# Order of the last feed-forward: steps written together, oldest group first, with a pause behind each combination of statistics

## The chip, the cores and the metric

The kernel runs on one core of one Trainium2 chip. Its time is the device time in microseconds of one execution, and the number that counts is the median of several runs. A separate execution under the hardware profiler gives the trace from which all durations here are taken.

## What is computed

The input is `x`, 4 images of 128 channels by 64 x 64 pixels. Layer 0 (a 1x1-convolution block with spatial attention) and the attention of layer 1 come first and take most of the time. What the change touches is the feed-forward half of layer 1 for the last image, for each of its 4096 tokens of 128 channels, cut here to what matters:

```python
def _ln(v, g, b):
    mu = jnp.mean(v, axis=-1, keepdims=True)
    var = jnp.mean((v - mu) ** 2, axis=-1, keepdims=True)
    return (v - mu) * jax.lax.rsqrt(var + EPS) * g + b
...
attn_out = ctx @ w_comb.T + b_comb
x1 = _ln(x + attn_out, g1, beta1)
zf = jnp.cos(x1[..., :NQ_FFN]) * jnp.cos(ry_theta)
h = jax.nn.relu(zf @ w1.T + b1)
ffn_out = h @ w2.T + b2
return _ln(x1 + ffn_out, g2, beta2)
...
t = t + _L1_attn_ref(...)
t = t + _L1_ffn_ref(_ln_t(t), ...)
```

So each token passes three normalisations (the two `_ln` and the `_ln_t` before the last layer), a cosine of its first eight channels, and four products (with `w_comb`, `w1`, `w2`, and `W` of the last layer). The last layer is a batch normalisation over all tokens of all images, followed by a recurrence in time, `y = sigmoid(wx + y @ V.T)`; it can't begin before the products with `W` of all tokens have gone into the statistics.

## The kernel before, in words

The four images go one after the other through a first stage (convolutions and layer 0), a second stage (attention), and feed-forwards that run beside the next image's first stage. The last image has no image behind it: its feed-forwards are a stage of their own, `last_stage` (from line 1680). Behind it comes the recurrence, which begins with `norm_of_products` (line 1494).

`last_stage` has eight groups of 512 tokens, each a generator made by `last_feed_forward` (line 1310). They are called A to H here, in the order in which they begin. A tile of a group is 128 partitions by 512, four blocks of 128 tokens. The steps of a group, with the engine and the tile names of the profile, are:

- loads of `x1` and `x0` on SyncE's queue, transposes `pc` on TensorE; `cT`, a copy on ScalarE (L1350); the product `pw` on TensorE (L1355); its addition to `x1` on VectorE (L1365);
- `parts`: four `bn_stats` on VectorE into `st` (L1322);
- `deviation` and the mean, on GpSimd: six small operations (L1329 to L1334, the last a power of -1/2) and one more, from `st` to `sv`, `rv` and `mv`;
- `both`: four normalising operations on VectorE that read `mv` (L1339);
- the chain of eight small VectorE operations on `z`, `zk`, `zr` (L1378 to L1391), the sine on ScalarE (L1393), a cast and a subtraction on VectorE (L1395, L1397), two copies into `zs` on ScalarE (L1402), transposes `pz` on TensorE, `zT` on ScalarE (L1409);
- twice the product `ph` on TensorE (L1416) and `hT` on ScalarE (L1426); then the 32 matmuls of `pf` on TensorE (L1432);
- `both` with `rv` and `pf` on VectorE; `parts`; the combination on GpSimd into `su`, `ru`, `mu`; `both` with `mu`; `both` with `ru`, which gives `t2`;
- `parts` of `t2` on VectorE and its transposes `pt` on TensorE; the combination on GpSimd into `sw`, `rw` and `less`, while ScalarE copies `t2T` (L1468) and SyncE stores it;
- the normalisation on ScalarE (L283), transposes `pl` on TensorE, the copy `last` on ScalarE (L1476), the product `pwx` on TensorE (L1489), `bn_stats` into `wx_stats` on VectorE (L1480) and the copy to `every` on ScalarE (L1482).

TensorE, ScalarE, VectorE and GpSimd execute their instructions here in the order in which the program writes them (`manual_schedule`). That order comes from a loop over ticks at the end of `last_stage`. Group k begins at tick `begins[k]`, and each active group goes one step further per tick; a tick is a matter of the order of writing and no barrier on the chip. Some pieces of the attention's end are written at the start of certain ticks (`between`): among them 16 copies each on ScalarE (ticks 2 and 8), on VectorE (tick 2) and on GpSimd (ticks 6 and 9, `xs` at L979), and joins on VectorE (ticks 4, 7 and 12).

Within a tick the groups take turns. A `yield 1` ends a group's step; a `yield 0` hands over to the next active group inside the same tick, so that `parts`, `both` and the small chains of several groups are written alternately, one VectorE instruction of each:

```python
on = list(active)
while on:
    for g in list(on):
        end = next(g, None)
        if end is None:
            active.remove(g)
        if end != 0:
            on.remove(g)
```

A group has 30 steps. GpSimd's combination is one step, and the VectorE or ScalarE instructions that read its result are the next. Tiles are taken from pools in turn: eight PSUM banks (`ps_one`), ten `fhalf`, six `hT`, eight of each small one.

Of the kernel before, what the change touches and what calls it, by code (L numbers as in the profile page):

```python
# [26 lines left out]
def kernel(  # L27
# [57 lines left out]
    here = {}  # L85
# [1224 lines left out]
    def last_feed_forward(im, i):  # L1310

        n, cols = im["n"], ts(i, IC)
        bits, _ = here["bits"]

        def bit(name, *shape):
            return bits.tile([P, *shape], F32, tag=name, name=f"{name}{n}_{i}")

        def parts(ap, st):  # L1320
            for k in range(TG):
                nc.vector.bn_stats(st[:, k, :], ap[:, ts(k, P)])  # L1322
                yield 0

        def deviation(st, sums, r):

            d = bit("d", TG)
            tt, each = nc.gpsimd.tensor_tensor, nc.gpsimd.tensor_scalar
            tt(sums, st[:, :, 1:3], st[:, :, 4:6], ALU.add)  # L1329
            tt(d, st[:, :, 1], st[:, :, 4], ALU.subtract)  # L1330
            tt(d, d, d, ALU.mult)
            each(r, sums[:, :, 1], 4.0 / P, 4e-5, ALU.mult, ALU.add)
            tt(r, r, d, ALU.add)
            tt(r, r, minus_half[:, 0:TG], ALU.pow)  # L1334

        def both(out, in0, factors, in1, op0, op1):
            for k in range(TG):
                at = ts(k, P)
                nc.vector.scalar_tensor_tensor(  # L1339
                    out[:, at], in0[:, at], factors[:, k : k + 1], in1(at), op0, op1  # L1340
                )
                yield 0

        x1, x0 = get("x1", f"lx1_{i}"), get("x0", f"lx0_{i}")
        nc.sync.dma_start(out=x1, in_=im["x1"][:, cols])
        nc.sync.dma_start(out=x0, in_=im["x0"][:, cols])
        pt = transposed(blocks(im["q"][:, cols]), f"pc{n}_{i}")
        yield 1
        cT = get("fhalf", f"cT{n}_{i}")
        nc.scalar.copy(cT, pt)  # L1350
        yield 1
        pa = one_psum(f"pw{n}_{i}")
        bias_first(pa, 1)
        for k in range(TG):
            nc.tensor.matmul(  # L1355
                pa[:, ts(k, P)],
                cT[:, ts(k, P)],
                wc_sb,
                start=False,
                stop=True,  # L1360
                skip_group_check=True,
            )
        yield 1
        v = x1
        nc.vector.tensor_tensor(v, pa, x1, ALU.add)  # L1365
        yield 1
        st = bit("st", TG, 6)
        yield from parts(v, st)
        yield 1
        sums, rv, mean = bit("sv", TG, 2), bit("rv", TG), bit("mv", TG)  # L1370
        deviation(st, sums, rv)
        nc.gpsimd.tensor_scalar(mean, sums[:, :, 0], 0.5, None, ALU.mult)
        yield 1

        yield from both(v, v, mean, lambda at: here["twice"][:, 0, :], ALU.subtract, ALU.mult)
        yield 1
        z, zk, zr = (bit(name, TG, D) for name in ("z", "zk", "zr"))
        nc.vector.tensor_tensor(  # L1378
            z, blocks(v)[:, :, 0:D], rv.unsqueeze(2).broadcast_to([P, TG, D]), ALU.mult
        )  # L1380
        yield 0
        nc.vector.tensor_tensor(z, z, be1_z.unsqueeze(1).broadcast_to([P, TG, D]), ALU.add)
        yield 0
        nc.vector.tensor_scalar(zk, z, 1.0 / (2 * math.pi), ROUND, ALU.mult, ALU.add)
        yield 0
        nc.vector.tensor_scalar(zk, zk, ROUND, None, ALU.subtract)
        for part, of in ((TWO_PI_1, z), (TWO_PI_2, zr), (TWO_PI_3, zr)):
            yield 0
            nc.vector.scalar_tensor_tensor(zr, zk, -part, of, ALU.mult, ALU.add)
        yield 0  # L1390
        nc.vector.scalar_tensor_tensor(zr, zr, -1.0, zr, ALU.mult, ALU.max)  # L1391
        yield 1
        nc.scalar.activation(zr, zr, AF.Sin, bias=half_pi, scale=-1.0)  # L1393
        yield 1
        nc.vector.tensor_copy(z.bitcast(F32R), zr)  # L1395
        yield 0
        nc.vector.tensor_tensor(zr, zr, z, ALU.subtract)  # L1397
        yield 1
        zs = get("fhalf", f"zs{n}_{i}")
        zv = zs.rearrange("p (k r y d) -> p k r y d", k=TG, y=2, d=D)  # L1400
        for y, part in enumerate((z, zr)):
            nc.scalar.copy(  # L1402
                zv[:, :, :, y, :], part.unsqueeze(2).broadcast_to([P, TG, P // (2 * D), D])
            )
        yield 1
        pz = transposed(blocks(zs), f"pz{n}_{i}")
        yield 1
        zT = get("fhalf", f"zT{n}_{i}")
        nc.scalar.copy(zT.bitcast(F32R), pz)  # L1409
        yield 1  # L1410
        hs = []
        for f0 in range(0, NF, 2):
            phs = [one_psum(f"ph{n}_{i}_{f}") for f in range(f0, f0 + 2)]
            hs.append(get("hT", f"hT{n}_{i}_{f0}"))
            for j in range(2):
                nc.tensor.matmul(  # L1416
                    phs[j],
                    f1_sb[:, f0 + j, :].bitcast(F32R),
                    zT.bitcast(F32R),
                    start=True,  # L1420
                    stop=True,
                )
            yield 1
            for j in range(2):
                bias = fb1_sb[:, f0 + j : f0 + j + 1]
                nc.scalar.activation(hs[-1][:, j, :], phs[j], AF.Relu, bias=bias)  # L1426
            yield 1
        po = one_psum(f"pf{n}_{i}")
        bias_first(po, 2)
        for k in range(TG):  # L1430
            for f in range(NF):
                nc.tensor.matmul(  # L1432
                    po[:, ts(k, P)],
                    hs[f // 2][:, f % 2, ts(k, P)],
                    f2_sb[:, f, :],
                    start=False,
                    stop=f == NF - 1,
                    skip_group_check=True,
                )
        yield 1  # L1440
        u = v
        yield from both(u, v, rv, lambda at: po[:, at], ALU.mult, ALU.add)
        yield 1
        st = bit("st", TG, 6)
        yield from parts(u, st)
        yield 1
        sums, r, mean = bit("su", TG, 2), bit("ru", TG), bit("mu", TG)
        deviation(st, sums, r)
        nc.gpsimd.tensor_scalar(mean, sums[:, :, 0], 0.5, None, ALU.mult)
        if i == NTG - 1:  # L1450
            nc.vector.tensor_tensor(blocks(x0), blocks(x0), row4(be2_bc), ALU.add)
        yield 1
        yield from both(u, u, mean, lambda at: here["twice"][:, 1, :], ALU.subtract, ALU.mult)
        yield 1
        t2 = x0
        yield from both(t2, u, r, lambda at: x0[:, at], ALU.mult, ALU.add)
        yield 1
        st = bit("st", TG, 6)
        yield from parts(t2, st)
        pt = transposed(blocks(t2), f"pt2_{n}_{i}")  # L1460
        yield 1
        sums, r, less = bit("sw", TG, 2), bit("rw", TG), bit("less", TG)
        deviation(st, sums, r)
        nc.gpsimd.tensor_tensor(less, sums[:, :, 0], r, ALU.mult)
        nc.gpsimd.tensor_scalar(less, less, -1.0, None, ALU.mult)
        nc.gpsimd.tensor_scalar(r, r, 2.0, None, ALU.mult)
        t2T = get("fhalf", f"t2T{n}_{i}")
        nc.scalar.copy(t2T, pt)  # L1468
        nc.sync.dma_start(out=t2_dram[im["rows"], cols], in_=t2T)
        yield 1  # L1470
        normalise_act(blocks(u), blocks(t2), less, r, TG)
        yield 1
        pt = transposed(blocks(u), f"pl{n}_{i}")
        yield 1
        tokens_i = get("fhalf", f"last{n}_{i}")
        nc.scalar.copy(tokens_i, pt)  # L1476
        yield 1
        pw = token_products(n, i, tokens_i)
        yield 1
        nc.vector.bn_stats(wx_stats[:, n * NIC + i, :], pw)  # L1480
        dst = held["every"][:, n, cols]
        nc.scalar.copy(  # L1482
            dst.rearrange("p (t c) -> p c t", t=L), pw.rearrange("p (c t) -> p c t", t=L)
        )
# [195 lines left out]
    def last_stage(im):  # L1680
# [28 lines left out]
        with stage(  # L1709
# [14 lines left out]
            while groups or active:  # L1724
                for f in between.get(tick, ()):
                    f()
                if groups and tick >= begins[NTG - len(groups)]:
                    active.append(groups.pop(0))
                on = list(active)
                while on:  # L1730
                    for g in list(on):
                        end = next(g, None)
                        if end is None:
                            active.remove(g)
                        if end != 0:
                            on.remove(g)
                tick += 1

    x_rows = x.rearrange("n c s -> (n c) s")
# [266 lines left out]
```

## Time and profile before

| | us |
|---|---|
| median of 3 runs (6988.06 to 6990.65) | 6988.64 |
| the profiled execution, its own time | 6989.88 |
| span of the profiled execution, first to last instruction | 6988.2 |
| busy in the span: TensorE / VectorE / ScalarE / GpSimd | 6812.8 / 5967.8 / 5932.7 / 2786.7 |
| last attention result of TensorE (L845) | up to about 6768.6 |
| first `wx_stats` of the last stage, last `wx_stats` of it (end) | 6846.7, 6892.4 |
| mean granted TensorE clock | 0.989 |

Times inside the trace count from the span's start. A line of the timeline gives start, duration, engine, line, operation, written and read tiles, shape, count, and in brackets the idle time before it and what ended that. Tile names leave out buffer numbers, and `lx` stands for the tiles of `x1`, `v`, `u`, `x0` and `t2`, which share buffers. A line of the waits view gives the waiting engine, tile and line, what it waited for, the total in us, how often, and the longest one.

### The profile page before, as it was taken

Reading aid. Unit: us, or ns where it says so; the run is one execution under the profiler, and the core shown is the slowest. Engines: PE = TensorE matmul, PEld = TensorE weight load, DVE = VectorE, ACT = ScalarE, POOL = GpSimd, SP = SyncE. Lnnn points to the kernel's source line nnn. Section 1 sums busy time; section 2 is a strip of 40 time slices with the busy share of each in tenths; the row PEclk is TensorE's granted clock in tenths of the full one; section 3 lists DMA queues with packets and bytes.
Section 4 is the critical chain, followed back from the end, with each engine's and each line's share of the span. In section 5 each row is a group of like instructions: output and inputs, shape, how many; then the busy total and the mean of one; then the engine's idle time right before and its main releaser. Section 6 shows DMA issues by size and latency. Waiting matters only on the chain. (4 is left out here: it accounts for less than half of the span.)

```text
span 6988.2 us, 223483 instructions
## 1 busy us (share of the span) xinstructions
PE 6812.8 (97%) x92333; PEld 3660.6 (52%) x92333; DVE 5967.8 (85%) x8064; ACT 5932.7 (85%) x11843; POOL 2786.7 (40%) x10008
## 2 busy tenths in 40 slices
PE   8999999999999999999999999999999999999996
PEld 4545555555664555555565455555466555555554
DVE  6688889987888999888787888888978888898987
ACT  4479999996669999999566999999956699999984
POOL 1134444434333444443433344444343434344442
PEclk9999999999999999999999999999999999999998
DMA  1110000000111000000111100000001100000012
GB/s 32 37 41 25 24 28 21 22 10 23 49 50 42 26 21 22 21 22 9 33 50 49 37 22 21 22 20 24 22 26 47 56 25 22 22 24 29 13 62 109
DMA packets 84760, 219.87 MB, mean 31 GB/s; under 512 B 9384, under 2 KB 10288, under 8 KB 82960
## 3 DMA queue, kind: packets, MB, share of 16 engines
q1 hardware_dynamic: 80448, 200.34, 8.4%
q8 instruction: 726, 11.89, 0.7%
q10 hardware_dynamic: 3024, 4.99, 0.2%
q14 instruction: 306, 2.51, 0.1%
q0 software_dynamic: 256, 0.13, 0.0%
HBM read 141.44 MB, written 56.62 MB: 28 GB/s over the span
## 5 line engine op out<-in xcount | busy, mean ns | idle before, releaser
L1069 ACT ACTIVATE e<-s 128x1024 f32<-128x1024 f32 (+1 forms) x3480 | 2950.0, 901 | 114.8 <-PE s L1057 83.0
L832 DVE STREAM_TRANSPOSE t<-e 128x1024 f32<-128x1024 f32 x2240 | 2594.2, 1210 | 77.3 <-ACT e L1069 74.6
L845 PEld LDWEIGHTS misc<-t,mirror 128*32 128x32 f32 x57344 | 1656.6, 110 | 1327.2 <-issue 1270.8
L845 PE MATMUL misc<-t,mirror 128*32 128x128 f32 x57344 | 1968.3, 273 | 18.6 <-DVE later L859 15.8
L1069 ACT ACTIVATE xs<-s 128x1024 f32<-128x1024 f32 (+1 forms) x2152 | 1838.9, 908 | 55.2 <-PE s L1057 43.0
L832 DVE STREAM_TRANSPOSE t<-xs 128x1024 f32<-128x1024 f32 x1344 | 1562.5, 1210 | 42.7 <-ACT xs L1069 41.2
L866 PE MATMUL acc<-e,q_aug 128*32 128x512 f32 x11360 | 1524.7, 609 | 1.0 <-POOL q_aug L748 1.0
L1057 PE MATMUL s<-queries,keys 32*128 32x512 f32 x9216 | 1243.2, 497 | 20.7 <-ACT e L1069 10.4
L912 POOL COPY own<-o 32x36 f32<-32x36 f32 x2048 | 430.7, 210 | 1807.1 <-DVE o L904 1727.1
L514 PE MATMUL acc<-p,asmT 128*128 128x512 f32 x2048 | 946.2, 593 | 1.8 <-DVE e L410 1.6
L866 PE MATMUL acc<-xs,q_aug 128*32 128x512 f32 x7072 | 942.4, 605 | 0.0
L507 ACT ACTIVATE p<-s 128x1024 f32<-128x1024 f32 x512 | 499.8, 1022 | 403.8 <-PE s L503 399.8
L1057 PEld LDWEIGHTS s<-queries,keys 32*128 32x128 f32 x9216 | 487.2, 182 | 601.4 <-issue 296.2
L937 POOL COPY other<-turned 32x64 f32<-32x64 f32 x1904 | 449.7, 236 | 624.3 <-DVE turned L927 545.8
L1069 ACT ACTIVATION_READ_ACCUMULATOR e<-s 128x1 f32 x2880 | 694.5, 241 | 0.0
L802 POOL COPY mirror<-q 32x128 f32<-32x128 f32 x2048 | 599.3, 293 | 199.2 <-PE misc L845 111.3
L503 PE MATMUL s<-hl,e 128*128 128x512 f32 x2048 | 586.4, 428 | 22.4 <-ACT p L507 10.9
L528 DVE TENSOR_TENSOR total<-total,p 128x1024 f32<-128x1024 f32 x448 | 547.8, 1223 | 22.0 <-ACT p L507 14.3
L514 PEld LDWEIGHTS acc<-p,asmT 128*128 128x128 f32 x2048 | 380.0, 190 | 334.8 <-issue 309.8
L503 PEld LDWEIGHTS s<-hl,e 128*128 128x128 f32 x2048 | 379.9, 189 | 178.3 <-issue 68.6
L1069 ACT ACTIVATION_READ_ACCUMULATOR xs<-s 128x1 f32 x1728 | 421.4, 244 | 0.0
L898 POOL COPY by_token<-by_key 32x4 f32<-32x4 f32 x2000 | 383.8, 192 | 84.4
(314 smaller groups left out, 4459.2 us busy)
## 6 DMA issues: line engine op xcount, KB each, us to landing
keys<-parts_dram SPq DMA_DIRECT2D x256, 256.0 KB
queries<-parts_dram SPq DMA_DIRECT2D x1024, 32.0 KB
x_dram<-x SPq DMA_DIRECT2D x56, 256.0 KB
fx<-x_dram SPq DMA_DIRECT2D x48, 256.0 KB
xs<-in_x_dram SPq DMA_DIRECT2D x16, 512.0 KB
t_dram<-t2T SPq DMA_DIRECT2D x32, 256.0 KB
t2s<-t_dram SPq DMA_DIRECT2D x16, 512.0 KB
hl<-hl SPq DMA_DIRECT2D x28, 256.0 KB
```

Of the source, the lines that this page charges most:

```text
L503: nc.tensor.matmul(s[:, j, :], stationary, moving, start=y == 0, stop=y == len(parts) - 1)
L507: nc.scalar.activation(p, s, AF.Exp)
L514: nc.tensor.matmul(state["acc", ic], asmT[:, ts(2 * jp + j, P)], p[:, j, :], start=jp == 0 and j == 0, stop=jp == NP - 1 and j == 1,)
L528: nc.vector.tensor_tensor(state[ic], state[ic], p, ALU.add)
L802: nc.gpsimd.tensor_copy(wv[ts(a, 32), s, :, :, ts(a, D)], own[ts(s, 32)])
L832: nc.vector.transpose(group["e"][h][:, k, :], es[h])
L845: nc.tensor.matmul(state["acc"][ts(2 * x + h, 32), :], state["w"][:, QT * (s // 4) + TG * x + s % 4, h, :], state["e"][h][:, :, ds(IC * x ...
L866: nc.tensor.matmul(it["in"]["acc"][ts(2 * h + x, 32), :], it["qa"][:, ds((2 * it["tiles"][x] + h) * V, 32)], it["e"][h][:, ts(x, IC)], sta ...
L912: nc.gpsimd.tensor_copy(own[ts(s, 32), ts(x, 4), h, :], ov[ts(2 * h + x, 32), s, :, 0:V])
L937: copy(to[ts(k, 32), h], tv[ts(2 * x + h, 32), k])
L1057: nc.tensor.matmul(ss[h][:, x, :], keys[unit[x] // QT].bitcast(F32R)[r, ts(unit[x] % QT, P)], queries[b].bitcast(F32R)[r, :], start=True, ...
L1069: nc.scalar.activation(es[h][:, ts(x, IC)] if split else es[h], ss[h][:, x, :] if split else ss[h].rearrange("p x c -> p (x c)"), AF.Exp, ...
```

## The change

Every `yield 0` goes, and each `yield 1` becomes a plain `yield`: what stands between two of them is written together. The loop lets each active group, the one that began first ahead of the others, go through one whole step per tick. Behind each of the three combinations on GpSimd a second `yield` is added, an empty step, so that a group has 33 steps and the instructions that read `mv`, `mu` and `rw` are written one tick later than before. `begins` and `between` stay as they are. No instruction is added, removed or changed. The transposes `pt`, which are in one step with `parts` of `t2`, were written behind four rounds of the tick and are now written with their group.

```diff
@@ -1320,7 +1320,6 @@
         def parts(ap, st):
             for k in range(TG):
                 nc.vector.bn_stats(st[:, k, :], ap[:, ts(k, P)])
-                yield 0
...
                 nc.vector.scalar_tensor_tensor(
                     out[:, at], in0[:, at], factors[:, k : k + 1], in1(at), op0, op1
                 )
-                yield 0
...
         st = bit("st", TG, 6)
-        yield from parts(v, st)
-        yield 1
+        parts(v, st)
+        yield
         sums, rv, mean = bit("sv", TG, 2), bit("rv", TG), bit("mv", TG)
         deviation(st, sums, rv)
         nc.gpsimd.tensor_scalar(mean, sums[:, :, 0], 0.5, None, ALU.mult)
-        yield 1
-
-        yield from both(v, v, mean, lambda at: here["twice"][:, 0, :], ALU.subtract, ALU.mult)
-        yield 1
+        yield
+        yield
+
+        both(v, v, mean, lambda at: here["twice"][:, 0, :], ALU.subtract, ALU.mult)
+        yield
...
-        yield 0
         nc.vector.tensor_tensor(z, z, be1_z.unsqueeze(1).broadcast_to([P, TG, D]), ALU.add)
-        yield 0
         nc.vector.tensor_scalar(zk, z, 1.0 / (2 * math.pi), ROUND, ALU.mult, ALU.add)
-        yield 0
...
         if i == NTG - 1:
             nc.vector.tensor_tensor(blocks(x0), blocks(x0), row4(be2_bc), ALU.add)
-        yield 1
-        yield from both(u, u, mean, lambda at: here["twice"][:, 1, :], ALU.subtract, ALU.mult)
-        yield 1
+        yield
+        yield
+        both(u, u, mean, lambda at: here["twice"][:, 1, :], ALU.subtract, ALU.mult)
+        yield
         t2 = x0
-        yield from both(t2, u, r, lambda at: x0[:, at], ALU.mult, ALU.add)
-        yield 1
+        both(t2, u, r, lambda at: x0[:, at], ALU.mult, ALU.add)
+        yield
         st = bit("st", TG, 6)
-        yield from parts(t2, st)
+        parts(t2, st)
         pt = transposed(blocks(t2), f"pt2_{n}_{i}")
-        yield 1
+        yield
...
         nc.sync.dma_start(out=t2_dram[im["rows"], cols], in_=t2T)
-        yield 1
+        yield
+        yield
         normalise_act(blocks(u), blocks(t2), less, r, TG)
...
                 if groups and tick >= begins[NTG - len(groups)]:
                     active.append(groups.pop(0))
-                on = list(active)
-                while on:
-                    for g in list(on):
-                        end = next(g, None)
-                        if end is None:
-                            active.remove(g)
-                        if end != 0:
-                            on.remove(g)
+                active = [g for g in active if next(g, active) is not active]
                 tick += 1
```

More of the change, by code (lines that the diff above doesn't have):

```diff
@@ L1380, in last_feed_forward @@
         )
-        yield 0
         nc.vector.tensor_tensor(z, z, be1_z.unsqueeze(1).broadcast_to([P, TG, D]), ALU.add)
-        yield 0
         nc.vector.tensor_scalar(zk, z, 1.0 / (2 * math.pi), ROUND, ALU.mult, ALU.add)
-        yield 0
         nc.vector.tensor_scalar(zk, zk, ROUND, None, ALU.subtract)
         for part, of in ((TWO_PI_1, z), (TWO_PI_2, zr), (TWO_PI_3, zr)):
-            yield 0
             nc.vector.scalar_tensor_tensor(zr, zk, -part, of, ALU.mult, ALU.add)
-        yield 0
         nc.vector.scalar_tensor_tensor(zr, zr, -1.0, zr, ALU.mult, ALU.max)
-        yield 1
+        yield
         nc.scalar.activation(zr, zr, AF.Sin, bias=half_pi, scale=-1.0)
-        yield 1
+        yield
         nc.vector.tensor_copy(z.bitcast(F32R), zr)
-        yield 0
         nc.vector.tensor_tensor(zr, zr, z, ALU.subtract)
-        yield 1
+        yield
         zs = get("fhalf", f"zs{n}_{i}")
@@ L1404, in last_feed_forward @@
             )
-        yield 1
+        yield
         pz = transposed(blocks(zs), f"pz{n}_{i}")
-        yield 1
+        yield
         zT = get("fhalf", f"zT{n}_{i}")
         nc.scalar.copy(zT.bitcast(F32R), pz)
-        yield 1
+        yield
         hs = []
@@ L1422, in last_feed_forward @@
                 )
-            yield 1
+            yield
             for j in range(2):
@@ L1426, in last_feed_forward @@
                 nc.scalar.activation(hs[-1][:, j, :], phs[j], AF.Relu, bias=bias)
-            yield 1
+            yield
         po = one_psum(f"pf{n}_{i}")
@@ L1439, in last_feed_forward @@
                 )
-        yield 1
+        yield
         u = v
-        yield from both(u, v, rv, lambda at: po[:, at], ALU.mult, ALU.add)
-        yield 1
+        both(u, v, rv, lambda at: po[:, at], ALU.mult, ALU.add)
+        yield
         st = bit("st", TG, 6)
-        yield from parts(u, st)
-        yield 1
+        parts(u, st)
+        yield
         sums, r, mean = bit("su", TG, 2), bit("ru", TG), bit("mu", TG)
@@ L1451, in last_feed_forward @@
             nc.vector.tensor_tensor(blocks(x0), blocks(x0), row4(be2_bc), ALU.add)
-        yield 1
-        yield from both(u, u, mean, lambda at: here["twice"][:, 1, :], ALU.subtract, ALU.mult)
-        yield 1
+        yield
+        yield
+        both(u, u, mean, lambda at: here["twice"][:, 1, :], ALU.subtract, ALU.mult)
+        yield
         t2 = x0
-        yield from both(t2, u, r, lambda at: x0[:, at], ALU.mult, ALU.add)
-        yield 1
+        both(t2, u, r, lambda at: x0[:, at], ALU.mult, ALU.add)
+        yield
         st = bit("st", TG, 6)
-        yield from parts(t2, st)
+        parts(t2, st)
         pt = transposed(blocks(t2), f"pt2_{n}_{i}")
-        yield 1
+        yield
         sums, r, less = bit("sw", TG, 2), bit("rw", TG), bit("less", TG)
@@ L1469, in last_feed_forward @@
         nc.sync.dma_start(out=t2_dram[im["rows"], cols], in_=t2T)
-        yield 1
+        yield
+        yield
         normalise_act(blocks(u), blocks(t2), less, r, TG)
-        yield 1
+        yield
         pt = transposed(blocks(u), f"pl{n}_{i}")
-        yield 1
+        yield
         tokens_i = get("fhalf", f"last{n}_{i}")
         nc.scalar.copy(tokens_i, pt)
-        yield 1
+        yield
         pw = token_products(n, i, tokens_i)
-        yield 1
+        yield
         nc.vector.bn_stats(wx_stats[:, n * NIC + i, :], pw)
```

## The prediction

> **What bounds the kernel now.** I read the windows view first, to size the stage that the change touches, then the waits inside it, then the timelines of VectorE (DVE), GpSimd (POOL) and TensorE. The stage runs from about 6770 us to the last `wx_stats` at 6892.43 us; behind it come the 94.5 us of the recurrence, which the change leaves alone. Columns: stretch, length, busy us of PE, PEld, DVE, ACT, POOL (with counts), granted clock, DMA share, GB/s.
> ```profile
> 6774.60:6893.50 118.90, 91.45 (x496) 72.45 (x495) 80.39 (x337) 66.16 (x143) 70.02 (x224) 0.77 0.23 91
> 6893.50:6988.00 94.50, 55.72 (x186) 29.42 (x186) 69.96 (x110) 36.47 (x93) 0.58 (x1) 0.81 0.45 172
> ```
> No engine is full in the stage, so waits decide. Here is the waits view of the stage.
> ```profile
> ACT every L1482 <- DVE wx_stats L1480: 18.3, 8, 3.5
> DVE lx L1339 <- POOL mu L1449: 13.8, 7, 3.4
> ...
> POOL sw L1329 <- DVE st L1322: 12.6, 6, 2.4
> ...
> DVE wx_stats L1480 <- PE pwx L1489: 10.1, 3, 3.6
> ...
> DVE lx L1339 <- POOL mv L1372: 7.1, 5, 2.4
> ...
> ACT lx L283 <- POOL rw L1466: 6.3, 2, 5.2
> ```
> VectorE and GpSimd wait for each other: VectorE 13.8 + 7.1 = 20.9 us for means from GpSimd (`mu`, `mv`), ScalarE 6.3 us for `rw`, and GpSimd 12.6 us for VectorE's `st`. The timelines of the two engines show the loop.
> ```profile
> 6854.40 0.22 POOL L1329 TENSOR_TENSOR sw<-st 128x8 f32<-128x8 f32 x1 [2.17 <-DVE st L1322]
> ...
> 6857.78 0.20 POOL L1329 TENSOR_TENSOR su<-st 128x8 f32<-128x8 f32 x1
> ...
> 6860.06 0.23 POOL L1449 TENSOR_SCALAR mu<-su 128x4 f32<-128x4 f32 x1
> ```
> ```profile
> 6852.27 0.35 DVE L1339 SCALAR_TENSOR_TENSOR lx<-lx,mu,twice 128x128 f32<-128x128 f32 x1 [2.13 <-POOL mu L1449]
> ...
> 6860.32 0.35 DVE L1339 SCALAR_TENSOR_TENSOR lx<-lx,mu,twice 128x128 f32<-128x128 f32 x1 [2.67 <-POOL mu L1449]
> ```
> From one `mu` to the next is 8.05 us: 2.1 us of VectorE up to the last `st`, then GpSimd's `sw` (3.4 us) and `su` (2.5 us) in series, for which VectorE stands still. The same eight microseconds lie at 6844.30 and 6868.30. At the end the last four groups follow at 4.33 us each (`wx_stats` at 6878.73, 6883.06, 6887.39, 6891.73): ScalarE's `every` 0.8 us, the next group's `last` 0.6, `pwx` 2.1 on a slow TensorE, `wx_stats` 0.7 and some 0.1 between them.
>
> **What the Trainium skill says.** "TensorE: Matmul & The Clock Gate", What's actually happening: the clock is halved after a mostly idle window of some 3.4 us and comes back after a busy one. The trace agrees; after TensorE sat 1.78 us for the first `pt`, the windows view has
> ```profile
> 6825.00:6828.00 3.00, 1.42 (x6) 0.82 (x7) 2.93 (x16) 2.15 (x5) 1.92 (x6) 1.00 0.00 0
> 6828.00:6831.00 3.00, 3.00 (x19) 3.00 (x18) 2.67 (x13) 0.79 (x2) 0.94 (x2) 0.61 0.25 93
> ```
> and that `pf` took 5.36 us where others take 3.73. A drop costs about 1.6 us. "VectorE: DVE Perf Modes", The DRAIN you can't avoid, says that chaining cannot skip the flush, and that an instruction that isn't held starts earlier. The trace has both: dependent small operations start 0.21 us apart (6786.38, 6786.59, 6786.81), interleaved with other groups' some 0.10 apart. "GPSIMD Engine Reference", Key points: GpSimd shares its SBUF interfaces with VectorE instructions of two SBUF inputs. The trace agrees: beside the 128x512 addition of L1451 a `sw` combination took 4.6 us instead of 3.3.
>
> **The change, part by part.** No instruction is added or removed; their order on VectorE, TensorE and ScalarE changes. A tick is no barrier, so an empty step costs nothing by itself.
>
> (1) *Steps together.* The small chain of `z` has eight operations. Alone it takes 1.67 us (6785.93 to 6787.60); interleaved it cost about 1.31 us (2.20 us from 6826.23 to 6828.43, less three big operations at 0.26 and one small at 0.11). The cast and subtraction cost 0.3 instead of 0.2. That is +0.45 us per group, and at most 8 x 0.45 = 3.6 us of VectorE, of which the first groups already pay. The big operations lose nothing: 0.20 us per `bn_stats`, 0.26 per normalising operation, in either order.
>
> (2) *The pause.* `mv`, `mu` and `rw` now have one further tick between GpSimd and their readers. VectorE's work then comes ahead: after the pause the even tick holds `ru` (1.04) and `parts` of u (0.80), the odd one `parts` of t2 (0.80), `mu` (1.04), `rv` (1.0), plus 0.6 for `wx_stats`; 5.3 us per two ticks. GpSimd needs 3.3 + 2.5 = 5.8. TensorE needs 5.55 while `pf` runs: `pf` 3.8, two `ph` 1.0, `pz` 0.35, `pt` 0.4. They overlap instead of adding up, so a two-tick round falls from 8.05 to about 5.6-6.4.
>
> (3) *`pt` moves ahead of the younger groups' TensorE work*, because it no longer comes after four rounds. It waits for the oldest group's `t2`. GpSimd's own queue keeps its order up to the first `su`; SyncE's only waiting issues are the eight stores of `t2T`, in the same order, and the 16 `t2s` loads wait for the end of the stage and shift with it.
>
> I followed the tick list engine by engine, in order, with those durations. Letters A to H are the groups.
> - Front. GpSimd's `sv` combinations and its two sets of 16 `xs` copies fill it from 6777.5 to 6794.8 in the old order. VectorE waits for the copies until 6785.0 as now, has A's normalisation and chain still to do, and is then full until `ru` of A at 6825.1. Before it waited some 6 us from there on (2.45, 0.36, 0.36, 0.34, 1.05, 1.76), but paid less for chains and had done A's normalisation inside the wait: A's `ru` started at 6825.85, and C's `rv` at 6829.25 where I now get 6825.1+1.04 = 6826.1. A gain of 1 to 3 us.
> - TensorE: `pf` of A, B, C at 6806.9, 6812.6, 6818.0 (now 6807.06, 6813.89, 6819.05). Then `pt` of A waits at the head of the queue from 6823.05 to 6824.8: one drop of clock, so D's `pf` ends at 6831.7 (now 6833.3).
> - From D on nothing waits for GpSimd. `pf` of E, F, G, H end at 6837.15, 6842.8, 6849.25 and 6854.75 (now 6840.88, 6847.99, 6854.37, 6861.26). ScalarE's 5.2 us at `rw` ahead of E's `hT` are gone.
> - Behind H's `pf`: `rv` 6855.0 to 6856.0, then in VectorE's order `ru` F, `parts` H, `parts` F, `mu` G, `wx_stats` C (1.04 + 0.8 + 0.8 + 1.04 + 0.6): C is done at 6860.3 (before: 6865.4).
> - Late next is the chain of 4.33 us per group, now for five groups rather than three: 6860.35 + 5 x 4.33 = 6882.0. Before: 6892.43. **Gain 10.4 us.**
> The profiled execution took 6989.88 us around its span of 6988.2, 1.24 above the median. 6989.88 - 10.4 = 6979.5; at the median 6988.64 - 10.4 = **6978.2 us**. Bounds of the parts that the trace doesn't show: the drop at `pt` costs 0 to 3.3 us (taken 1.6, one such drop seen); handovers I took at 0.1 to 0.25 us, as seen, and another 0.1 on some thirty of them makes 3 us. So 6975 to 6983 for this case. GpSimd has slack of 1.3 us (`su` of H, done 6860.8, wanted about 6862) to 5 us.
>
> **Rivals.**
> - *GpSimd stays the bound* (0.18). Five `sw` and six `su` lie between A's `sw` and H's `mu`. At 3.2 and 2.5 they take 31 us; at the 4.6 seen beside VectorE's two-input addition for each `sw`, 7 us more, less 1.3 of slack: 5.7 us late, **6984**. For: VectorE's normalising operations have two inputs and now run without gaps. Against: the page of the kernel before has such a slow `sw` once in eight.
> - *TensorE stays fast in the tail* (0.14). `pwx` then takes 1.0 instead of 2.1, five times: 5 us less, **6973**. For: `pt`, `pl`, `pwx` now lie together. Against: from 6866 to 6893 the clock was 0.50, with a busy share like that expected.
> - *Slower: `pt` at the head of TensorE's queue waits in every round* (0.10). Then each of D to H pays about 1 us of gap and 1.7 us of half clock: 5 x 2.7 = 13.5 us, **6992**, above today. It decides if VectorE's `ru` ends more than about a microsecond after TensorE is through, thus if VectorE needs more than 5.6 + 1 per two ticks; I count 3.6 to 5.3.
> - *Nothing gained* (0.06): the longer small chains in a full VectorE until 6826 take what the pauses give, **6988**.
>
> **How the numbers follow.** The likeliest case has 0.52 and gives the time. The range from 6971 to 6990 takes in the rivals but the slower one, and leaves some 0.15 outside. A measurement of this kernel can tell about 0.2% from no change, 14 us: under 6974.7 lies the fast tail, 0.14; above 7002.6 only a worse form of the slower rival, 0.04; the rest is 0.82.
>
> **What would show it.** Right: the waits of L1339 for `mu` and `mv` nearly gone; `mu` rounds of 5.6 to 6.4 us; `pf` of H ending near 6855; `wx_stats` 4.33 us apart from the third group on; stage end near 6882. Step (1) shows in the `z` chains, 1.67 us without a foreign instruction between. Wrong: `mu` still waiting, GpSimd without gaps (the first rival), or a clock of 0.5 between 6832 and 6855 with `pt` waiting for L1339 (the third).

## The result, and the profile after

The changed kernel takes 6975.85 us (median of 15 runs, 6973.11 to 6979.97), the kernel before 6988.06 us (15 runs, 6984.30 to 6990.65). The ratio is 0.9982, with a 95% interval of 0.9976 to 0.9989: 12.2 us less. The profiled execution took 6976.16 us around a span of 6974.4 us, against 6989.88 around 6988.2.

Totals of this kernel scatter by some 3 to 4 us to either side, and the work ahead of the last feed-forward has a part in it: in the traces below the stage begins between 6773.5 and 6779.0 us. Most of what follows is therefore read from the trace as **the stage**: from the first addition of `pw` on VectorE to the end of the last `wx_stats`. Two profiled executions of the changed kernel gave 105.64 and 105.69 us for it. In the kernel before it is 117.82 us (6774.61 to 6892.43).

The windows view of the changed kernel shows the stage and what is behind it, in the columns that the prediction names.

```profile
6774.46:6880.10 105.64, 83.09 (x494) 68.26 (x494) 80.94 (x336) 65.31 (x142) 68.60 (x224) 0.83 0.26 99
6880.10:6974.40 94.30, 55.95 (x188) 29.20 (x186) 70.80 (x111) 37.59 (x94) 0.58 (x1) 0.81 0.45 174
```

VectorE's busy time is about what it was (79.36 us before, from the same view with the same bounds): the stage is 12.18 us shorter because VectorE stands idle less (24.7 us instead of 38.5). The rest behind it, 94.30 us against 95.77, isn't touched by the change; in the other executions below it lies between 93.5 and 95.7 us.

The waits view of the stage in the changed kernel has no line in which VectorE waits for `mu` or `mv`, nor one in which ScalarE waits for `rw`; before these were 13.8, 7.1 and 6.3 us. Four of the lines that are left:

```profile
DVE wx_stats L1475 <- PE pwx L1484: 12.8, 4, 3.6
...
ACT every L1477 <- DVE wx_stats L1475: 8.8, 6, 2.9
...
DVE lx L1338 <- PE pf L1425: 4.0, 5, 1.3
...
PE pt L291 <- DVE lx L1338: 3.0, 1, 3.0
```

The first two lie mostly in the tail, in which each group's `wx_stats` waits for its `pwx`. The last is one wait of `pt` at the head of TensorE's queue, which the change brought.

How the loop of VectorE and GpSimd opened shows in their timelines. GpSimd first, in the changed kernel:

```profile
6847.28 0.22 POOL L1442 TENSOR_SCALAR mu<-su 128x4 f32<-128x4 f32 x1
6847.48 0.19 POOL L1328 TENSOR_TENSOR sw<-st 128x8 f32<-128x8 f32 x1
```

And VectorE:

```profile
6846.07 1.11 DVE L1338 SCALAR_TENSOR_TENSOR lx<-lx,mu,twice 128x128 f32<-128x128 f32 x4
...
6848.29 1.12 DVE L1338 SCALAR_TENSOR_TENSOR lx<-lx,rv,pf 128x128 f32<-128x128 f32 x4 [1.11 <-PE pf L1425]
...
6852.53 1.13 DVE L1338 SCALAR_TENSOR_TENSOR lx<-lx,mu,twice 128x128 f32<-128x128 f32 x4
```

The `mu` that GpSimd finishes at 6847.50 is read at 6852.53, 5 us later; `sw` starts as soon as `mu` is through, with no wait for `st`. VectorE now waits for TensorE's `pf` instead, and for less. From one `mu` on VectorE to the next is 6.46 us here, where it was 8.05.

Where the stage got shorter can be read group by group from the ends of `wx_stats`, counted from the stage's start:

| | A | B | C | D | E | F | G | H |
|---|---|---|---|---|---|---|---|---|
| before, us | 72.8 | 80.8 | 90.9 | 97.8 | 104.8 | 109.1 | 113.5 | 117.8 |
| after, us | 70.9 | 77.4 | 84.8 | 88.3 | 92.6 | 97.0 | 101.3 | 105.6 |
| gained, us | 1.9 | 3.4 | 6.1 | 9.6 | 12.2 | 12.2 | 12.2 | 12.2 |

All is gained by the fifth group. The three behind it still follow at 4.33 to 4.35 us each, as before. VectorE's timeline of the changed kernel has `wx_stats` of C, D, E and F:

```profile
6858.56 0.68 DVE L1475 BATCH_NORM_STATS2 wx_stats<-pwx 128x6 f32<-128x512 f32 x1
6862.03 0.68 DVE L1475 BATCH_NORM_STATS2 wx_stats<-pwx 128x6 f32<-128x512 f32 x1
6866.38 0.70 DVE L1475 BATCH_NORM_STATS2 wx_stats<-pwx 128x6 f32<-128x512 f32 x1 [1.84 <-PE pwx L1484]
6870.73 0.70 DVE L1475 BATCH_NORM_STATS2 wx_stats<-pwx 128x6 f32<-128x512 f32 x1 [3.65 <-PE pwx L1484]
```

C to D is only 3.47 us, then 4.35: D's `pwx` ran at full clock in 1.12 us, E's took 2.07. TensorE's timeline has both, and the gap that lies ahead of them:

```profile
6860.78 1.12 PE L1484 MATMUL pwx<-last,WT_sb 128*128 128x512 f32 x2 [3.53 <-ACT last L1471]
6864.27 2.07 PE L1484 MATMUL pwx<-last,WT_sb 128*128 128x512 f32 x2 [0.62 <-ACT last L1471]
```

### The profile page after: what moved, and what is told of

Same layout as the page of the kernel before. It is cut to its first block, busy times and chain, and to the rows that moved or that the text cites. A ratio compares the mean times of both kernels' runs of the same rounds, so it can differ in the third digit from the quotient of the medians.

```text
span 6974.4 us, 223486 instructions
## 1 busy us (share of the span) xinstructions
PE 6808.2 (98%) x92333; PEld 3655.8 (52%) x92333; DVE 5966.9 (86%) x8064; ACT 5937.1 (85%) x11843; POOL 2795.6 (40%) x10008
## 3 DMA queue, kind: packets, MB, share of 16 engines
q10 hardware_dynamic: 3024, 4.99, 0.2%
## 5 line engine op out<-in xcount | busy, mean ns | idle before, releaser
L503 PE MATMUL s<-hl,e 128*128 128x512 f32 x2048 | 587.7, 428 | 21.0 <-ACT hl L465 11.1
```

The lines of the kernel that those rows point to most:

```text
L503: nc.tensor.matmul(s[:, j, :], stationary, moving, start=y == 0, stop=y == len(parts) - 1)
```

## The experiments

Each was run beside the kernel before on one chip; e1 to e4, e0 with e5 to e7, and e8 to e11 are three sets on three chips. The table has what the traces show of each: the stage, the end of E's `wx_stats` from the stage's start (the loop), the time from there to the end of the stage (the tail of F, G, H), and VectorE's waits for `mu` and `mv` and ScalarE's for `rw`. Each stage is that of one trace. The gain in the median and the gain of the stage differ by 2.2 us at most.

| kernel | median, before beside it, us | ratio (95%) | stage | E done | tail | `mu` / `mv` / `rw` |
|---|---|---|---|---|---|---|
| before | – | – | 117.8 | 104.8 | 13.0 | 13.8 / 7.1 / 6.3 |
| after | 6975.85, 6988.06 | 0.9982 (0.9976–0.9989) | 105.6 | 92.6 | 13.0 | 0 / 0 / 0 |
| e0, after again | 6976.62, 6989.84 | 0.9981 (0.9974–0.9988) | 105.7 | 92.7 | 13.0 | 0 / 0 / 0 |
| e1, together only | 6977.12, 6989.61 | 0.9982 (0.9974–0.9989) | 103.1 | 92.9 | 10.2 | 3.1 / 4.2 / 4.4 |
| e2, pause only | 6974.38, 6989.61 | 0.9979 (0.9970–0.9988) | 104.2 | 92.1 | 12.1 | 4.4 / 0 / 0 |
| e3, `pt` later | 6977.01, 6989.61 | 0.9980 (0.9972–0.9989) | 103.3 | 93.2 | 10.2 | 4.7 / 0 / 2.7 |
| e4, `every` later | 6973.84, 6989.61 | 0.9978 (0.9969–0.9986) | 101.1 | 91.0 | 10.1 | 0 / 0 / 2.5 |
| e5, only `parts` of t2 first | 6980.52, 6989.84 | 0.9987 (0.9981–0.9994) | 108.0 | 96.9 | 11.1 | 4.1 / 7.1 / 5.3 |
| e6, e2 and `every` later | 6974.03, 6989.84 | 0.9978 (0.9970–0.9986) | 102.2 | 89.5 | 12.7 | 4.4 / 0 / 5.9 |
| e7, e1 and `every` later | 6975.09, 6989.84 | 0.9980 (0.9973–0.9988) | 101.8 | 92.9 | 8.9 | 3.1 / 4.4 / 7.6 |
| e8, e3 and e4 | 6977.29, 6991.62 | 0.9980 (0.9972–0.9988) | 102.1 | 91.0 | 11.1 | 4.4 / 0 / 9.4 |
| e9, TensorE kept busy | 6974.26, 6991.62 | 0.9975 (0.9966–0.9985) | 101.9 | 91.7 | 10.2 | 0 / 0 / 0 |
| e10, e9 and e4 | 6974.51, 6991.62 | 0.9976 (0.9966–0.9985) | 100.7 | 90.8 | 9.8 | 0 / 0 / 1.1 |
| e11, e2, e5 and `every` later | 6973.20, 6991.62 | 0.9973 (0.9963–0.9984) | 100.7 | 88.2 | 12.5 | 1.6 / 0 / 4.0 |

**The changed kernel again (e0).**

> The kernel after, unchanged, as the base for the others of this call. 0.998 of the kernel before; from the first addition of pw to the last wx_stats 105 to 106 us, as in its first profile (105.6), if TensorE's clock is halved in the last five groups as it was there; 3 to 4 us less if it is not.

It measured 0.9981, and its stage is within 0.05 us of the first. Other pairs agree less well. E2 and e6 have the same instructions up to the first `wx_stats`, yet A's `ru` begins 46.99 us into the stage in one and 46.27 in the other; e4 is the changed kernel up to there, and its A is done 0.4 us later. So a difference of stage of less than about a microsecond isn't read as an effect here, unless the two traces agree up to the place of the edit. Totals of two versions a few microseconds apart overlap in their intervals.

**Order and pause apart (e1, e2).** The changed kernel without the three added empty steps, and the kernel before with them:

```diff
  # e1, against the changed kernel, at all three places
         yield
-        yield
```

```diff
  # e2, against the kernel before, at all three places
         yield 1
+        yield 1
```

> Steps written together, oldest group first, without the three pauses. Theory of the prediction (the pauses remove the waits for mu and mv): the waits of L1338 for mu and mv come back, 15 to 20 us of them, and the gain is mostly gone: 6983 to 6990 us, last wx_stats at 6888 us or later. Rival (the order alone breaks the loop): written oldest first, parts of t2 of the older group stand ahead of the wait for mu, so GpSimd can do sw while VectorE waits; a round is then su and sw in series on GpSimd, 5.8 us instead of 8.05, and four rounds save 9 us: 6977 to 6981 us, with mu still waited for but less than 2 us a time.

> The three pauses alone; within a tick the groups still take turns, one VectorE instruction each. Theory: the pauses bring the gain and writing together costs some (0.45 us per group for the small chains, and the transposes pt at the head of TensorE's queue, 3.0 us of gap and a slow clock behind it in the kernel after): as fast as the kernel after or up to 4 us faster, 6972 to 6976 us, last wx_stats at 6876 to 6880 us, no gap of TensorE ahead of the first pt. Rival (turns are what hurts: rv waiting for pf in the first round holds every other group's instructions): 6980 us or more.

Each alone gives about the whole gain: E is done at 92.9 and 92.1 us, with both at 92.6. For e1 the theory on record, that the gain would mostly go, failed, and its rival came; for e2 the theory held. Both stages are even shorter than that of the changed kernel (103.1 and 104.2 against 105.6), by tails in which the last `pwx` ran at full clock (F, G and H in e1, H in e2). Writing together alone leaves waits for the means, as these lines of its waits view show,

```profile
DVE lx L1338 <- POOL mv L1370: 4.2, 2, 2.1
...
DVE lx L1338 <- POOL mu L1441: 3.1, 4, 1.4
```

but they are a third of what they were, 7.3 us against 20.9. The two parts take away the same wait, so their gains don't add up. It shows on GpSimd too: `sw` waited for `st` six times before, 12.6 us in all, and 3.3 us in e1; in e2, where `mu` is ready when VectorE comes to it, so that the `bn_stats` behind it aren't held up, there is one such wait, 4.1 us, and in the changed kernel one of 4.3. The cost of writing together is there too: A's `ru` begins 49.47 us after the stage's start in the changed kernel and 46.99 in e2.

**Which line of the order it is (e5).** In the kernel before, `bn_stats` of `t2` of an old group and the four normalisations with `mu` of a younger one were dealt out in turn, and the older group's `sw` on GpSimd needs the last of these `bn_stats`. This kernel is the kernel before with only these four written together, ahead of the younger group's instructions:

```diff
         st = bit("st", TG, 6)
-        yield from parts(t2, st)
+        for _ in list(parts(t2, st)):
+            yield 0
```

> The kernel before with one thing changed: the four bn_stats of t2 are written together, in the first round of their tick, ahead of the younger groups' normalisations with mu; no pause, everything else in turns. Theory after the first runs (what costs 8 us a round before is that the bn_stats of t2 are dealt out between the normalisations that wait for mu, so that sw can't start while VectorE waits): the rounds fall to 5.8 to 6.5 us, VectorE's wait for mu from 13.8 to under 5 us, the stage from 117.8 to 107 to 110 us, the time by 8 to 11 us. Rival (the order of the other steps matters as much, or the pause does): less than 4 us gained.

The stage is 9.8 us shorter (108.0), as expected: 7.9 us at the end of E, and 1.9 in the tail, where `pwx` of G and H ran at full clock. The wait for `mu` falls to 4.1 us, while that for `mv` stays as it was. E5's waits view:

```profile
DVE lx L1339 <- POOL mv L1372: 7.1, 5, 2.5
...
DVE lx L1339 <- POOL mu L1449: 4.1, 3, 2.0
```

GpSimd's timeline of it shows the mechanism:

```profile
6844.29 0.23 POOL L1449 TENSOR_SCALAR mu<-su 128x4 f32<-128x4 f32 x1
6844.48 0.20 POOL L1329 TENSOR_TENSOR sw<-st 128x8 f32<-128x8 f32 x1
```

`sw` starts 0.19 us after `mu`. In the lines of the kernel before that stand in the prediction, VectorE's first normalisation with `mu` began at 6852.27, and `sw` only at 6854.40, after a wait of 2.17 us for `st`: the last `bn_stats` that it needed stood in VectorE's queue behind an instruction that waited for `mu`. With them ahead of it, `sw` and VectorE's normalisation overlap.

**`pt` later (e3, e8).** The changed kernel, with the transposes `pt` one step later and the copy of `t2T` in the empty step; e8 has the edit of e4 as well.

```diff
         parts(t2, st)
-        pt = transposed(blocks(t2), f"pt2_{n}_{i}")
         yield
...
         nc.gpsimd.tensor_scalar(r, r, 2.0, None, ALU.mult)
+        pt = transposed(blocks(t2), f"pt2_{n}_{i}")
+        yield
         t2T = get("fhalf", f"t2T{n}_{i}")
...
         yield
-        yield
         normalise_act(blocks(u), blocks(t2), less, r, TG)
```

> The kernel after, with the transposes pt of a group one step later, beside its combination on GpSimd, and t2T in the step that was empty. Theory (step 3 of the prediction, pt at the head of TensorE's queue costs a gap and a drop of the clock): the gap of 3.0 us ahead of the first pt goes and D's pf takes 3.7 instead of 4.7 us; VectorE is full up to 6830 us and its waits for pf behind that are 4.0 us in all, so 2 to 4 us are gained: 6972 to 6974 us. Rival (VectorE is the bound there anyway, the gap is hidden): 6975 to 6977 us.

> The kernel after with pt one step later and the copy to every one step later. Theory (pt later brings D's and E's pf 5.6 us forward, of which GpSimd's su and sw in series leave 1.2 us at C's wx_stats; every later saves 3 to 4 us behind that; they add): stage 105.7 - 1.2 - 3.5 = 101 us at a half clock, 100 with the clock full at the end. Rival (what GpSimd gives last is the bound of the end): no shorter than with every later alone, 101.1 us.

The gap is gone and D's `pf` runs at full clock. TensorE's timeline in the changed kernel and in e3, in this order:

```profile
6824.33 1.26 PE L291 MATMUL pt<-ident,lx 128*128 128x128 f32 x4 [3.03 <-DVE lx L1338]
...
6825.82 4.74 PE L1425 MATMUL pf<-f_sb,hT 128*128 128x128 f32 x32
```

```profile
6825.76 3.73 PE L1425 MATMUL pf<-f_sb,hT 128*128 128x128 f32 x32
```

D's `pf` ends 50.6 us into the stage instead of 56.1. Yet E is done at 93.2 us, not earlier than the 92.6 of the changed kernel, for VectorE waits for `mu` again (4.7 us). One line of e3's VectorE:

```profile
6844.09 1.14 DVE L1338 SCALAR_TENSOR_TENSOR lx<-lx,mu,twice 128x128 f32<-128x128 f32 x4 [1.51 <-POOL mu L1442]
```

The theory on record, 2 to 4 us less, failed, and its rival came: GpSimd is the next bound there. That e3's stage is 2.3 us shorter comes from the tail, where `pwx` of F, G and H ran at full clock (1.12 or 1.13 us). With `every` later in both, the later `pt` gains nothing either (e8 102.1, e4 101.1), where 101 or less was expected. So the gap ahead of the first `pt` is hidden: taking it away moved TensorE's work, and not the end of the loop.

**`every` later (e4, e6, e7).** In the tail, ScalarE's copy `every` of one group stands ahead of the next group's `last`. One added step puts it behind:

```diff
         nc.vector.bn_stats(wx_stats[:, n * NIC + i, :], pw)
+        yield
         dst = held["every"][:, n, cols]
```

e6 is e2 with this, e7 is e1 with it.

> The kernel after, with the copy of a group's products to every one step later than its bn_stats, so that ScalarE does the next group's last before it. Theory (the end of the stage is the chain every, last, pwx, wx_stats of 4.33 us a group): the distance of the last four wx_stats falls to about 3.6 us, what TensorE's pwx, pl and pt and the copy last take at half clock, and 2 to 3 us are gained: 6972.5 to 6974 us. Rival (TensorE at half clock or the normalisation on ScalarE sets the 4.33 us): the distance stays and the time is 6975 to 6977 us.

> The pauses alone, groups in turns, and the copy to every one step later. Theory (the two gains lie in different stretches and add up): the stage 104.2 - 3 = 101 us, the time 0.9975 of the kernel before or less. Rival (the end of the stage is then set by TensorE's clock or by VectorE's order): within 1 us of the pauses alone, 0.9979.

> Written together without pauses, and the copy to every one step later. The stage took 103.1 us with the copy in its old place, with TensorE at full clock at its end and the last three wx_stats 3.39 us apart. Theory (that chain is every, last, pwx, wx_stats at either clock): the distance falls to 2.6 to 3 us and the stage to 100 to 102 us. Rival (GpSimd's su and sw in series, 5.8 us a round, last until the end and hide the chain): 102.5 to 103.5 us.

It takes 4.6 us off the stage of the changed kernel (101.1), where 2 to 3 were expected, 2.0 off e2 (102.2, where 101 was expected), of which 0.7 lie ahead of the edit, and 1.3 off e1, as expected. D to E is then 2.43 us. VectorE's timeline in e4, `wx_stats` of D and E:

```profile
6862.46 0.68 DVE L1475 BATCH_NORM_STATS2 wx_stats<-pwx 128x6 f32<-128x512 f32 x1
...
6864.89 0.67 DVE L1475 BATCH_NORM_STATS2 wx_stats<-pwx 128x6 f32<-128x512 f32 x1
```

The same order made the gap of 3.53 us ahead of D's `pwx`. ScalarE's timeline of the changed kernel has C's `every`, which waits for VectorE, and D's `last` behind it:

```profile
6859.27 1.02 ACT L1477 COPY every<-pwx 128x512 f32<-128x512 f32 x1 [2.37 <-DVE wx_stats L1475]
6860.10 0.62 ACT L1471 COPY last<-pl 128x512 f32<-128x512 f32 x1
```

With `every` later D's `last` doesn't wait for it. TensorE's timeline of e4, D and E:

```profile
6857.92 1.12 PE L1485 MATMUL pwx<-last,WT_sb 128*128 128x512 f32 x2 [0.24 <-ACT last L1471]
...
6861.29 1.12 PE L1485 MATMUL pwx<-last,WT_sb 128*128 128x512 f32 x2 [0.20 <-ACT last L1471]
```

The gap is gone, and E's `pwx` ran at full clock too. F's took 2.08 us, behind a wait of ScalarE for `rw` (2.5 us), so E to F is 4.51 us. So the step of 4.33 us was a loop through ScalarE's order as well as through the clock.

**TensorE kept busy (e9, e10).** The changed kernel with matmuls that nobody reads behind the transposes `pt` of F (14), G and H (4 each). e10 has the edit of e4 as well.

```diff
         pt = transposed(blocks(t2), f"pt2_{n}_{i}")
+        place = GROUPS.index(i)
+        if place >= NTG - 3:
+            fill = one_psum(f"fill{n}_{i}")
+            for k in range(14 if place == NTG - 3 else 4):
+                nc.tensor.matmul(
+                    fill[:, ts(k % TG, P)], ident, wc_sb, start=True, stop=True, skip_group_check=True
+                )
         yield
```

> The kernel after with work added that nobody reads: 14 matmuls 128x128x128 behind the pt of group F, 4 behind those of G and H, into a bank of their own. Theory (the last groups are 4.34 us apart because TensorE stands idle for 3.5 us ahead of D's pwx and then runs at half clock): pwx takes 1.1 instead of 2.1 us, the last five wx_stats are 3.4 us apart, the stage falls from 105.7 to 102 us. Rival (the distance is set by ScalarE and VectorE, or the added matmuls delay pwx): 105 to 107 us.

> The same added matmuls (nobody reads them) and the copy to every one step later. With every later alone the last distances were 3.47, 2.43, 4.51, 2.65, 2.87 us. Theory: at a full clock the 4.51 falls to about 2.6 and the stage from 101.1 to 99 us. Rival (the 4.51 is a wait for rw, which the clock doesn't touch): 100.5 to 101.5 us.

The stage is 3.7 us shorter (101.9), as expected. The first 14 fill the stretch in which TensorE stood idle. TensorE's timeline of e9:

```profile
6858.66 3.29 PE L1459 MATMUL fill<-wc_sb,ident 128*128 128x128 f32 x28
6862.38 1.12 PE L1491 MATMUL pwx<-last,WT_sb 128*128 128x512 f32 x2 [0.43 <-ACT last L1478]
...
6876.05 1.12 PE L1491 MATMUL pwx<-last,WT_sb 128*128 128x512 f32 x2 [1.52 <-ACT last L1478]
```

The windows view gives the clock in the third figure from the end, of the changed kernel from the gap on and then of the tail of e9:

```profile
6857.00:6861.00 4.00, 0.47 (x4) 0.23 (x3) 4.00 (x18) 1.73 (x3) 3.46 (x14) 1.00 0.17 66
6861.00:6863.00 2.00, 2.00 (x8) 1.17 (x8) 2.00 (x8) 1.98 (x6) 1.75 (x4) 0.76 0.00 0
6863.00:6880.00 17.00, 13.00 (x30) 6.77 (x29) 4.24 (x11) 11.11 (x22) 6.72 (x24) 0.50 0.22 77
```

```profile
6866.00:6877.90 11.90, 7.97 (x33) 4.25 (x33) 2.90 (x5) 9.58 (x20) 5.48 (x18) 1.00 0.26 89
```

The groups follow at 3.38 to 3.42 us instead of 4.33 to 4.35, and four such steps make the 3.7 us. With `every` later too the stage is 100.7 us, so of the 4.6 us of e4 only 1.3 remain: e4 and e9 shorten the same chain. The 99 us of the theory for e10 weren't reached; E to F is still 3.60 us. What the order is worth at full clock shows between D and E: 3.42 us in e9 and 2.43 in e10.

**The best of both (e11).** The kernel before with the pauses of e2, the edit of e5, and `every` later.

> Pauses, groups in turns, but the bn_stats of t2 written together in the first round of their tick, and every one step later. Theory (in turns the front is 2.5 us shorter; what remains behind it is GpSimd's sw, which starts late because the bn_stats of t2 are dealt out): the waits for mu and rw of 4.4 and 5.9 us fall by half and the stage from 102.2 to 99 to 100.5 us. Rival (GpSimd is full there, 5.8 us a round, and an earlier st changes nothing): 101.5 to 102.5 us.

The stage of 100.7 us lies between the 99 to 100.5 of the theory and the 101.5 of its rival. E11 has the earliest E of all (88.2 us), for it pays nothing for chains written together (A's `ru` at 47.05 us) and has no `mv` wait, and the lowest ratio, 0.9973. Its tail is slow: `pwx` of F, G and H took 2.07 or 2.08 us (12.5 us in all). Its stage is 5.0 us shorter than that of the changed kernel. In total times the intervals of the two overlap (0.9963 to 0.9984 against 0.9976 to 0.9989), so that it beats the kernel before is shown, and that it beats the changed kernel is shown for the stage only, in one trace.

## Why the prediction was right, and where it was wrong

**The number** held: a gain of 10.4 us was forecast and 12.2 measured; the end of the stage was put at 6882.0 and came at 6880.10. As forecast, that is within 0.2% (14 us) of the kernel before, though the interval shows that less than 0.2% can be told from no change. That the number held doesn't tell whether the pause was its cause: with either part alone E is done at about the same time.

**Step 1, together.** The `z` chain alone was put at 1.67 us and took 1.66 (6811.81 to 6813.47). The cost in the first groups, bounded by 3.6 us, measured 2.5 at A's `ru`. What failed is the role given to this step. The prediction counted only a cost for it and gave the gain to the pause. E1 and e5 show that the order by itself overlaps `sw` with VectorE's `mu`, and that one line of it is worth 7.9 us up to E. The prediction had read the right lines, `sw` starting 2.1 us after VectorE's `mu`, but put this down to GpSimd and VectorE working in series, and missed that it was the dealing out that put the `bn_stats` behind the waiting instruction.

**Step 2, the pause.** Right in what it does: waits for `mu`, `mv` and `rw` are nil, and e2 gains 13.65 us of stage with it alone, though 4.4 us of waits for `mu` remain there. The `mu` rounds were put at 5.6 to 6.4 us; on VectorE they measure 5.90, 6.39, 6.71, 6.17, 6.46, 4.99 and 3.46, the first six 6.10 in the mean.

**Step 3, `pt` at the head.** It waits, and once: the third rival, a wait in every round, didn't come. The gap was put at 1.75 us and measured 3.03, since TensorE was through with the work ahead of it at 6821.30, not 6823.05; D's `pf` took 4.74 us, 1.0 over the usual 3.73, where 1.6 was taken; a further part of the drop fell on `pt` itself (1.26 us, later ones 0.60). E3 adds that the loop is not longer for it.

**The sum.** The end was missed by 1.9 us, in two terms. The first is 1.1 us at D's `pf`. Somewhat less than half of it is `pt`, put at 6824.8 and begun at 6824.33. That forecast did not fit the prediction's own A's `ru` at 6825.1, for `pt` reads what `ru` writes; in the trace `ru` began at 6823.93, and `pt` 0.4 us behind it. Kept in order, the forecast would have come out some 0.7 us later. The rest is the stretch from the start of `pt` to the end of D's `pf`, 6.2 us instead of 6.9. Part of this is luck: e0, e4, e9 and e10 have the same instructions in the same order up to there, and it took 6.28, 6.55, 6.26 and 6.41 us, for the clock fell at a different point. From there on the 1.1 us came through: D to H's `pf` ended at 6830.6, 6836.2, 6841.8, 6848.3 and 6853.8, each about 1 us earlier than forecast (H: 6854.75), and C's `wx_stats` at 6859.24 instead of 6860.35. The second term is D, which followed at 3.47 instead of 4.33 us, since the clock fell only behind D's `pwx`; with the other four steps 0.06 us longer in all, it is 0.8 us. Two small misreadings enter no sum: C was done at 6865.51 before, not 6865.4, and 95.77 us lie behind the stage, not 94.5.

**The rivals.** GpSimd as the bound didn't show in the changed kernel, but in e1 and e3 VectorE waits for it again. Its price of 4.6 us for each `sw` rests on a reading that doesn't hold as it stands: in the kernel before, the operations of the slow `sw` took 0.33 to 0.38 instead of 0.20 us from 6837.10 on, 2 us before the addition of L1451 began, so the addition can't be the whole reason; in the changed kernel the `sw` beside that addition took 3.8 us and the others 3.1 to 3.5.

The fast tail, with 0.14, came in e9, and for the last two or three groups in e1, e3 and e5, but not in the changed kernel: in it TensorE has 0.47 us of work between 6857 and 6861, and behind that stretch the clock fell. There D's `last` stands behind C's `every` on ScalarE, which waits for a full VectorE (4.00 of 4.00 us). E4 and e9 take this gap away in two ways, and in both E's `pwx` ran at full clock. "TensorE: Matmul & The Clock Gate", Why this matters for your kernels, warns of idle gaps above some 3 us between bursts; the trace agrees with its gap of 3.53 us, after which the clock went from 1.00 to 0.76 and then 0.50. It isn't the least that does it: in the kernel before, which the prediction took for agreement with the page's 3.4 us, the wait was 1.78 us, TensorE was busy for 1.42 of 3.00 us around it, and the clock fell all the same. What sets whether a tail is fast without fillers, as it is in e1 and e3, was not settled; e9 shows only that filling this gap and the two smaller ones behind it is enough here.

## What to carry to other kernels

Where engines wait for each other in a ring, look at what stands in an in-order queue behind the instruction that waits: work that another engine needs goes ahead of it, which here was worth 7.9 us of the loop with four `bn_stats` of each group moved, and took a gap of 3.5 us from TensorE with one copy of each group moved on ScalarE. Two edits that each remove the same wait count once, so try each alone before keeping both. When totals scatter more than the effect, measure the stage from the trace, and split it (here the loop and the tail) before giving a gain to a cause.

## What was not expected of the hardware

5.4 us of matmuls that nobody reads (3.29, 1.06 and 1.06 us in e9's trace) made the stage 3.7 us shorter. The busy share alone doesn't tell when the clock falls. In e1 TensorE was busy for 59% of this stretch, and kept its clock nearly to its end:

```profile
6857.00:6865.00 8.00, 4.76 (x22) 2.57 (x20) 6.84 (x26) 4.81 (x10) 6.83 (x25) 0.98 0.17 64
```

and in the tail of e9 67% of busy time went with a clock of 1.00, while in the changed kernel 76% went with 0.50, because each matmul took about twice as long. In the changed kernel the clock lost behind the gap of 3.53 us stayed lost for the 17 us that were left. In e1, where only E's `pwx` was slow (2.08 us, then three times 1.13), and in e3 (D and E slow behind a gap of 3.47 us, then 1.12 or 1.13) it came back; no run here tells why. The order of the instructions doesn't settle it: e1 and e7 have the same order up to the first `wx_stats`, and D's `pf` took 3.73 us in one and 5.36 in the other. The fast tails of e1, e3 and e5 are seen in one trace each.
